# A four-layer graph kernel: new planned costs for TensorE's mode changes, and a new set of priorities for its planner

## The chip, the cores and the metric

The kernel runs on one core of one Trainium2 chip. The metric is the device time of one launch in microseconds (us). A core has five engines that run their own instruction streams and wait for one another through semaphores: TensorE (PE; its weight loads are listed as PEld) multiplies matrices, VectorE (DVE) and ScalarE (ACT) work element by element, GpSimd (POOL) does small work and issues DMAs, SyncE (SP) issues DMAs.

## The reference

32 independent graphs of 512 nodes with 256 features pass through four layers. Each layer is `x = layernorm(x + layer(x, adj))`:

- Layer 0: `h = (1+eps)*x + adj @ x`, then `relu(h @ W1 + b1) @ W2 + b2` with 512 hidden features.
- Layer 1: attention with 4 heads of 64 features. The score is `leaky_relu(e_dst[i] + e_src[j])` where `adj > 0.5`, masked elsewhere; softmax; times `h = x @ W`; plus a bias.
- Layer 2: attention with 8 heads of 32 features, `softmax(q k^T / sqrt(32) + log(adj + 1e-6))` times `v`, then an output projection with bias.
- Layer 3: `softmax` over nodes of `((x @ W) @ x^T) * adj` with a node mask, times `x`.

Everything is float32; 512 nodes are four chunks of 128, 256 features are two chunks of 128.

## The kernel before

**Tiling.** Each graph is computed by some 375 small steps, each with a name, an engine and a planned duration. In layer 0 they are `at` (adj transposed by TensorE, L679), `h` (adj @ x, L712), `f` and `y` (the two products of the layer, L735, L754). In layer 1: `xt1` (x transposed, L782), `v1` (L803), `z` (ACT, L906) and `zm` (DVE, L917) that make the weights, `o1` (weights times values, L940), `ad` (the four chunks of the weights added up by accumulating DMAs that POOL issues, L968), `d1` (the denominators out of them, L988), `yt`, `dt` (small transposes, L1017, L1018, L1005). In layer 2: `q`, `k` (L1073), `v2` (L1091) with its eviction `ve2` (ACT, L1097), `s` (scores of four heads at once, L1110), `e` (exponentials on ACT, L1123), `m` (times adj, DVE, L1132), `cd` (accumulating DMAs, L1143), `n` (weights times values of four heads at once, L1168), `d2` (denominators, L1198), `p` (projection, L1253). In layer 3: `i` (L1297), `t` (L1311), `te` (exponentials, L1341), `u` (transposes, L1350), `w` (L1365). The additions of biases to x are `xb` (POOL, L581), the reciprocal roots of the layer norms `dev` (POOL, L607). `la` and `lb` are the loads of adj for layer 0 and for layer 3.

**Modes of TensorE.** Most steps use the whole 128 x 128 array. Some use parts of it at the same time: `s` splits the rows in four (mode "row", 32 rows each), `n`, `d2` and `d1` split the columns in four (mode "c32"), `o1` splits the columns in two (mode "c64"). The others have mode "".

**Order.** The order of all instructions of all engines comes from a planner that runs while the program is built (class `Plan`). It replays the steps of all graphs with planned durations, and at each turn looks for those that could start first. Among the steps that can start within `ahead` of the earliest it takes the one with the smallest due time:

```
due = turn[g] * period - self.left[g][name] + moved[name] + stay * change
```

`left` is the planned length of the longest chain that follows the step, `period` is 28 (us per graph), `moved` holds shifts of single kinds of steps in us (before: the sum of 14 seeded random draws that each touch some 15% of the kinds), and `change` is the planned duration of the change of mode in front of a TensorE step, from the table `CHANGE`, weighted by `stay`. Up to six graphs (`window`) are in work at a time. Buffers are limited by a stock: 11 big tiles, 12 middle ones, 17 strips, and the eight PSUM banks ("p": 8), of which one `s` step takes four. What the planner hands out is only an order and a buffer for each tile: on the chip every engine runs its stream in that order, and semaphores hold an instruction until its operands are there. Planned times have no effect on the chip beyond the order and the choice of buffers.

Of the kernel before, what the change touches and what calls it, by code (L numbers as in the profile page):

```python
# [46 lines left out]
class Plan:  # L47
# [6 lines left out]

    HOP = {"pe": 0.2, "act": 0.15, "dve": 0.13, "pool": 0.05, "sp": 0.05}
    BACK = {"act": 0.13, "dve": 0.12}

    CHANGE = {  # L60
# [4 lines left out]
    }  # L65

    def __init__(self, stock):
# [64 lines left out]
            t = max(t, ends[h][n] + self.hop(self.steps[h][n], s))  # L132
        return t

    def order(self, period, ahead, window, stay, shifts=(), rush=()):


        room = {b: [(0.0, i) for i in range(n)] for b, n in self.stock.items()}
        engine, mode, out, last = {}, "", [], 0.0
        held = [{} for _ in self.steps]  # L140
        ends = [{} for _ in self.steps]
        waits = [{n: len(s.after) for n, s in steps.items()} for steps in self.steps]
        fwaits = [[len(after) for _, after in frees] for frees in self.frees]
        ready, low, opened = {}, 0, 0
        todo = [len(steps) for steps in self.steps]
        moved = dict.fromkeys((n for steps in self.steps for n in steps), 0.0)
        turn = [max(g - 1, 0) for g in range(len(self.steps))]
        for i, early in enumerate(rush):
            turn[-1 - i] -= early
        for seed, far in shifts:  # L150
            rng = random.Random(seed)
            for n in moved:
                if rng.random() < 0.15:
                    moved[n] += rng.uniform(-far, far)

        def open_to(n):
            nonlocal opened
            while opened < min(n, len(self.steps)):
                for name in self.steps[opened]:
                    if not waits[opened][name]:  # L160
                        ready[opened, name] = self.ready(opened, name, ends)
                opened += 1

        open_to(window)
        while low < len(self.steps):
            found = []
            for (g, name), t in ready.items():
                s = self.steps[g][name]
                t = max(t, engine.get(s.eng, 0.0))
                change = self.CHANGE[mode][s.mode] if s.eng == "pe" else 0.0  # L170
                for k, (kind, _, rest) in enumerate(s.take):
                    r, n = room[kind], sum(b[0] == kind for b in s.take[:k])
                    if len(r) <= rest + n:
                        break
                    t = max(t, r[n][0])
                else:
                    due = turn[g] * period - self.left[g][name] + moved[name] + stay * change
                    found.append((t, due, g, name, change))
            if not found:
                return math.inf, out  # L180
            first = min(found)[0] + ahead
            _, t, g, name, change = min((due, t, *f) for t, due, *f in found if t <= first)
            s = self.steps[g][name]
            t += change
            if s.eng == "pe":
                mode = s.mode
            del ready[g, name]
            got = {}
            for kind, key, _ in s.take:
                got[key] = held[g][key] = (kind, room[kind].pop(0)[1])  # L190
            if s.eng:
                engine[s.eng] = t + s.us
            end = ends[g][name] = t + s.us
            last = max(last, end)
            out.append((g, name, t, got))
            for h, n in s.then:
                waits[h][n] -= 1
                if not waits[h][n] and h < opened:
                    ready[h, n] = self.ready(h, n, ends)
            for k in s.frees:  # L200
                fwaits[g][k] -= 1
                if not fwaits[g][k]:
                    key, after = self.frees[g][k]
# [21 lines left out]
def fast_path(  # L225
# [102 lines left out]
    def prepare():  # L328
# [23 lines left out]
        def transposed(name, w):  # L352
            def raw():
                t[f"raw{name}"] = mid(f"raw{name}", [P, DC, D])
                return t[f"raw{name}"], rows(w)

            load(f"raw{name}", 2.0, raw, take=(f"C=raw{name}",))

            @step(f"wt{name}", "pe", 0.44, (f"raw{name}",), take=(f"p=wt{name}",))
# [12 lines left out]
            @step(f"we{name}", "act", 0.49, (f"wt{name}",), free=(f"wt{name}",))  # L372
            def _():
                nc.scalar.copy(wT[name].rearrange("p c f -> p (c f)"), t[f"wt{name}"])
# [36 lines left out]
                    prod.rearrange("p c (h f) -> p c h f", h=H1), AX.X, ALU.add,  # L411
                )

        @step("wtg", "pe", 0.44, ("wg",), take=("p=wtg",))
# [139 lines left out]
    def graph(g):  # L554
# [111 lines left out]
        for c in range(NC):  # L666

            @step(
                f"at{c}", "pe", 0.44, (f"la{c}",) + prev("at", c),
                take=(f"p=at{c}",) + (() if c else ("AT=ATcap", "B=AT/4", "D=ATd")),  # L670
            )
            def _(c=c):
                if c == 0:
                    t["AT"] = big("AT", [P, NC, N], "AT")

                    t["ATd"] = strip("ATd", [P, NC, P], "ATd")
                pt = t[f"pt{c}"] = bank(f"at{c}", [P, NC, P], f"AT_t_{c}")
                for m in range(NC):
                    nc.tensor.transpose(pt[:, m, :], t[f"A{c}"][:, blk(m)], ident)  # L679
# [88 lines left out]
        for d in range(DC):  # L768

            @step(  # L770
                f"xt1{d}", "pe", 0.44, row("r1", NC) + prev("xt1", d),
                take=(f"p=xt1{d}",) + (() if d else ("L1", "C=xT1/1")),
            )
            def _(d=d):
# [267 lines left out]
        def features_first(n, more=()):  # L1042
            for d in range(DC):

                @step(
                    f"xt{n}{d}", "pe", 0.44, row(f"r{n}", NC) + prev(f"xt{n}", d),
                    take=(f"p=xt{n}{d}",) + (() if d else (f"C=xT{n}",) + more),
                )
                def _(d=d):
# [49 lines left out]
        def scores(k):  # L1099
            o, c = divmod(k, NC)  # L1100

            @step(
                f"s{k}", "pe", 0.87, (f"qe{o}", f"ke{o}") + prev("s", k),
                take=tuple(f"p=s{k}{j}" for j in range(4)), mode="row",
            )
            def _():
# [49 lines left out]
        def attend(k):  # L1156
            o, c = divmod(k, NC)

            @step(
                f"n{k}", "pe", 0.87,  # L1160
                (f"m{k}1",) + ((f"n{k-1}",) if k else row("qe", 2) + row("ke", 2) + row("ve2", NC)),
                take=(f"p=n{o}",) if c == 0 else (), mode="c32",
            )
# [141 lines left out]
        for c in range(NC):  # L1305
# [37 lines left out]
                    accum_out=t["den"][:, c : c + 1],  # L1343
                )

            @step(f"u{c}", "pe", 0.44, (f"te{c}",) + prev("u", c), take=(f"p=u{c}",), free=(f"z3{c}",))
# [63 lines left out]
    for g in range(B):  # L1410
        graph(g)
    with tc.manual_schedule():
        plan.run([(28, 0.05, 6, 75.0, ((824592, 5.0), (893565, 10.0), (244737, 10.0), (911503, 5.0), (695937, 2.0), (23294, 5.0), (391254, 2.0), (207664, 2.0), (760101, 2.0), (339516, 5.0), (335230, 2.0), (34898, 2.0), (376325, 5.0), (379301, 2.0)), (0.6, 0.0, 0.1))])

# [470 lines left out]
```

## Time and profile before

| | us |
|---|---|
| median of 3 runs | 2972.07 (2971.11 to 2972.57) |
| profiled execution | 2974.01 |
| its span, first to last instruction | 2972.2 |
| granted TensorE clock, mean | 0.997 |
| busy: TensorE, DVE, ACT, POOL | 2929.2, 2127.1, 1918.8, 776.0 |

The profile shows one execution. Busy time of an engine is the time in which it has an instruction running; idle time of an engine is listed with what ended it. L735 is line 735 of the kernel. An operation in float32 of TensorE stands as two records for each matmul of the program, and records of matmuls in parts of the array start some nanoseconds apart and run together. The ends of matmuls are modelled, so the distance from one start to the next is the better measure of their pace.

### The profile page before, as it was taken

What the parts mean: (1) busy time and instruction counts of PE and PEld (TensorE: products, weight loads), DVE (VectorE), ACT (ScalarE), POOL (GpSimd) and SP (SyncE); (2) the same over time, 40 slices, a digit from 0 to 9 for tenths busy, and PEclk for the clock granted to TensorE, in tenths of its full rate; (3) what the DMA queues carried; (4) which work ended last, traced back from release to release, by engine and by line L of the source; (5) the groups of instructions that cost most, each with busy time, mean ns of one, the idle gap of its engine ahead of it and who ended that gap; (6) DMA issues with size and microseconds to landing.
All of it is one profiled execution on the core that took longest, in us unless ns stands there. A gap on an engine that the chain in (4) does not pass through costs nothing.

```text
span 2972.2 us, 42591 instructions
## 1 busy us (share of the span) xinstructions
PE 2929.2 (99%) x15521; PEld 1662.6 (56%) x15521; DVE 2127.1 (72%) x4133; ACT 1918.8 (65%) x3818; POOL 776.0 (26%) x688
## 2 busy tenths in 40 slices
PE   8899999999999999999999999999999999999998
PEld 6445555555555555555555555555565555555444
DVE  2577767776777777777767677767777776766886
ACT  3665766657666667666566666576666675656664
POOL 1333222232222222222222222222222222222220
PEclk9999999999999999999999999999999999999999
DMA  4677576676766676866777766768666766766770
GB/s 145 133 165 169 147 164 139 154 155 162 175 145 139 149 176 151 177 134 151 151 170 167 151 142 153 167 153 181 137 147 142 178 159 135 162 133 141 165 156 19
DMA packets 153368, 448.93 MB, mean 151 GB/s; under 512 B 15232, under 2 KB 55360, under 8 KB 125248
## 3 DMA queue, kind: packets, MB, share of 16 engines
q0 software_dynamic: 63648, 295.73, 52.3%
q1 hardware_dynamic: 88112, 149.75, 15.0%
q8 instruction: 125, 2.05, 0.3%
q10 hardware_dynamic: 1392, 0.66, 0.1%
q14 instruction: 91, 0.75, 0.1%
HBM read 133.30 MB, written 17.07 MB: 51 GB/s over the span
## 4 chain that ended last, share of the span: by engine, by line
PE 91%; DVE 3%; ACT 3%; DMA 2%; issue 1%; POOL 0%; POOLq 0%; ACTq 0%
PE s L1110 9%; PE h1T_ps L735 8%; PE o_ps L1168 8%; PE o_ps L940 7%; PE hT_ps L712 7%; PE o_ps L1365 7%; PE s L1311 7%; PE y_ps L754 7%; PE v_ps L803 4%; PE iT_ps L1297 4%; PE o2p_ps L1253 4%; PE v_ps L1091 4%; PE qT_ps L1073 3%; PE kT_ps L1073 3%; PE d_ps L1198 2%; PE eT_t L1350 2%
## 5 line engine op out<-in xcount | busy, mean ns | idle before, releaser
L1132 DVE SCALAR_TENSOR_TENSOR z<-AT,z 128x1024 f32<-128x1024 f32 x512 | 621.5, 1229 | 235.1 <-ACT z L1123 232.3
L1123 ACT ACTIVATE z<-s 128x512 f32<-128x512 f32 x1024 | 571.2, 606 | 99.2 <-PE s L1110 98.4
L917 DVE SCALAR_TENSOR_TENSOR z<-z,T,edge 128x512 f32<-128x512 f32 x512 | 412.4, 857 | 10.6 <-ACT z L906 10.1
L906 ACT ACTIVATE z<-R_bc,nT,S 128x512 f32<-128x512 f32 x512 | 382.9, 807 | 8.9 <-DMA R_bc<-R_dram 5.2
L1143 POOL DMA_DIRECT2D z<-z x186 | 164.9, 919 | 785.2 <-PE o_ps L1168 211.9
L968 POOL DMA_DIRECT2D z<-z x256 | 227.1, 1063 | 472.7 <-DMA z<-z 239.6
L581 POOL TENSOR_TENSOR x<-x,bias_bc 128x1024 f32<-128x1024 f32 x96 | 238.9, 2489 | 382.0 <-PE hT_ps L712 160.3
L1217 DVE RECIPROCAL rdT<-rdT 128x256 f32<-128x256 f32 x128 | 215.5, 1723 | 166.7 <-ACT rdT L1210 166.6
L625 ACT ACTIVATE x<-x,shift,rstd 128x256 f32<-128x256 f32 x508 | 289.6, 599 | 19.6 <-DVE shift L615 19.6
L1110 PE MATMUL s<-qT,kT 32*128 32x512 f32 x2048 | 294.9, 638 | 1.1 <-DVE y L1023 0.6
L607 POOL TENSOR_TENSOR rstd<-ve,nhalf 128x4 f32<-128x4 f32 (+1 forms) x131 | 144.5, 1146 | 545.3 <-DVE ve L601 530.0
L1168 PE MATMUL o_ps<-z,v 128*32 128x512 f32 x2048 | 264.2, 601 | 0.3 <-DVE z L1132 0.3
L940 PE MATMUL o_ps<-z,v 128*64 128x512 f32 x1024 | 237.8, 603 | 8.7 <-DVE z L917 8.7
L735 PE MATMUL h1T_ps<-hT,w_sb 128*128 128x512 f32 x512 | 245.6, 605 | 0.1
L1365 PE MATMUL o_ps<-x,eT 128*128 128x256 f32 x1024 | 237.6, 380 | 1.4 <-ACT eT L1355 1.3
L1311 PE MATMUL s<-xT,iT 128*128 128x512 f32 x512 | 238.9, 599 | 0.0
L754 PE MATMUL y_ps<-w_sb,h1T 128*128 128x256 f32 x1024 | 226.3, 379 | 0.0
L1365 PEld LDWEIGHTS o_ps<-x,eT 128*128 128x128 f32 x1024 | 193.3, 190 | 55.2 <-issue 19.0
L584 DVE BATCH_NORM_STATS2 st<-x 128x6 f32<-128x256 f32 x508 | 211.8, 417 | 7.9
L1341 ACT ACTIVATE z<-z,nmax 128x512 f32<-128x512 f32 x128 | 92.4, 722 | 193.2 <-DVE nmax L1333 191.7
L754 PEld LDWEIGHTS y_ps<-w_sb,h1T 128*128 128x128 f32 x1024 | 194.2, 190 | 38.5 <-issue 12.7
L712 PE MATMUL hT_ps<-AT,x 128*128 128x384 f32 (+2 forms) x768 | 211.5, 385 | 0.0
(152 smaller groups left out, 4192.0 us busy)
## 6 DMA issues: line engine op xcount, KB each, us to landing
z<-z POOLq DMA_DIRECT2D x186, 1024.0 KB, 9.1
A<-in_adj_dram SPq DMA_DIRECT2D x256, 256.0 KB
z<-z POOLq DMA_DIRECT2D x128, 512.0 KB, 7.1
R_bc<-R_dram SPq DMA_DIRECT2D x32, 1024.0 KB
z<-z POOLq DMA_DIRECT2D x128, 256.0 KB, 5.2
x<-in_x_dram SPq DMA_DIRECT2D x32, 512.0 KB
out_dram<-x SPq DMA_DIRECT2D x31, 512.0 KB
nm<-in_nodemask_dram SPq DMA_DIRECT2D x32, 256.0 KB
```

The source lines that it names most:

```text
L712: nc.tensor.matmul(ph[:, cols], t["x"][:, m, blk(d)], moving, start=(k == 0), stop=(k == len(parts) - 1),)
L735: nc.tensor.matmul(ph, w1_sb[:, d, blk(f)], t["hT"][:, d, :], start=(d == 0), stop=(d == DC - 1))
L754: nc.tensor.matmul(py[:, j, :], t["h1T"][:, f, blk(2 * c2 + j)], w2_sb[:, f, :], start=(f == 0), stop=(f == HC - 1),)
L906: nc.scalar.activation(t[f"e{h}"][:, c, :], t["Rbc"][:, h, :], AF.Relu, bias=t["nT"][:, h, c : c + 1], scale=t["S"][:, h, c : c + 1],)
L917: nc.vector.scalar_tensor_tensor(z, z, t["T"][:, h, c : c + 1], t["edge"][:, c, :], op0=ALU.add, op1=ALU.mult)
L940: nc.tensor.matmul(po[j * F1 : (j + 1) * F1, :], t["v"][:, c, h * F1 : (h + 1) * F1], t[f"e{h}"][:, c, :], start=(c == 0), stop=(c == NC - 1),
L1110: nc.tensor.matmul(pk, t["k"][hs, o, blk(c)], t["q"][hs, o, :], start=True, stop=True)
L1123: nc.scalar.activation(t[f"E{k}"][:, j, :], t[f"ps{k}{j}"], AF.Exp, scale=QSCALE)
L1132: nc.vector.scalar_tensor_tensor(z, t["AT"][:, c, None, :].to_broadcast([P, 2, N]), ADJ_EPS, z, op0=ALU.add, op1=ALU.mult,)
L1168: nc.tensor.matmul(t[f"n{o}"][32 * j : 32 * j + 32, :], t["v2"][:, c, o * P + F2 * j : o * P + F2 * (j + 1)], t[f"E{k}"][:, j, :], start=( ...
L1311: nc.tensor.matmul(pt, t["iT"][:, d, blk(c)], t["xT3"][:, d, :], start=(d == 0), stop=(d == DC - 1),)
L1365: nc.tensor.matmul(py, t[f"eT{c}"][:, blk(m)], t["x"][:, m, :], start=(m == 0), stop=(m == NC - 1),)
```

## The change

Three things change, all of them inputs of the planner.

1. Planned durations. The table of changes of mode gets other values (0.13 to 0.10, 0.17 to 0.218 and so on); the packed steps `s`, `n` and `d2` are planned with 0.855 instead of 0.87 us, transposes of four chunks with 0.437 instead of 0.44.
2. `order` takes a further argument, `moves`: a list of step kinds and of shifts in us, which are added to `moved`. 308 kinds are in it.
3. The arguments of the one run: `ahead` 0.05 to 0.0, `stay` 75 to 55, ten of the 14 seeded draws are replaced, the head start of the last graphs is 0.5, 0, 0 periods instead of 0.6, 0, 0.1.

No instruction is added or removed, and no operand but the choice of buffers differs.

```diff
     CHANGE = {
-        "": {"": 0.0, "row": 0.13, "c32": 0.1, "c64": 0.1},
-        "row": {"": 0.17, "row": 0.1, "c32": 0.2, "c64": 0.2},
-        "c32": {"": 0.12, "row": 0.12, "c32": 0.0, "c64": 0.12},
-        "c64": {"": 0.12, "row": 0.12, "c32": 0.12, "c64": 0.0},
+        "": {"": 0.0, "row": 0.1, "c32": 0.1, "c64": 0.09},
+        "row": {"": 0.218, "row": 0.11, "c32": 0.218, "c64": 0.218},
+        "c32": {"": 0.13, "row": 0.12, "c32": 0.02, "c64": 0.14},
+        "c64": {"": 0.118, "row": 0.118, "c32": 0.067, "c64": 0.0},
     }
...
-    def order(self, period, ahead, window, stay, shifts=(), rush=()):
+    def order(self, period, ahead, window, stay, shifts=(), rush=(), moves=()):
...
+        for n, far in moves:
+            moved[n] += far
         for seed, far in shifts:
...
-                f"at{c}", "pe", 0.44, (f"la{c}",) + prev("at", c),
+                f"at{c}", "pe", 0.437, (f"la{c}",) + prev("at", c),
...
-                f"s{k}", "pe", 0.87, (f"qe{o}", f"ke{o}") + prev("s", k),
+                f"s{k}", "pe", 0.855, (f"qe{o}", f"ke{o}") + prev("s", k),
...
-                f"n{k}", "pe", 0.87,
+                f"n{k}", "pe", 0.855,
...
-                f"d2{o}", "pe", 0.87 * len(chunks),
+                f"d2{o}", "pe", 0.855 * len(chunks),
...
-        plan.run([(28, 0.05, 6, 75.0, ((824592, 5.0), (893565, 10.0), (244737, 10.0), (911503, 5.0), ...), (0.6, 0.0, 0.1))])
+        plan.run([(28, 0.0, 6, 55.0, ((824592, 5.0), (893565, 10.0), (244737, 10.0), (23294, 5.0), ...), (0.5, 0.0, 0.0), (
...
+('ad00', -62.0), ('ad01', -61.5), ('ad10', -77.0), ('ad11', -51.5), ('ad20', -67.0), ('ad21', -32.5), ('ad30', -65.0), ('ad31', -48.0),
...
+('at1', -36.0),
...
+('e00', -46.5), ('e02', -5.0), ('e03', 10.0), ('e10', -34.0), ('e12', -1.0), ('e13', -2.0), ('e20', -1.0), ('e21', -9.0), ('e22', -95.0), ('e23', -32.0),
...
+('h0', -21.0), ('h1', -29.5),
...
+('i0', 27.5),
...
+('k0', -33.0),
...
+('la0i', -32.0), ('la1i', -33.5), ('la2i', 20.0), ('la3i', 2.0),
...
+('lb0i', -35.0), ('lb1i', -5.0), ('lb2i', -37.0), ('lb3i', -15.0),
...
+('o100', -38.5),
...
+('oe0', 21.5), ('oe1', 78.5),
...
+('s1', -36.0),
...
+('v23', -35.5),
...
+('ve10', 30.0), ('ve11', 10.0), ('ve12', 22.0), ('ve13', 31.5), ('ve20', 117.0), ('ve21', 58.0), ('ve22', 1.0), ('ve23', 6.5),
...
```

The same 0.44 to 0.437 stands at the other transposes (`wt`, `wtg`, `xt1`, `xt2`, `xt3`, `u`).

More of the change, by code (lines that the diff above doesn't have):

```diff
@@ L357, in transposed @@
             load(f"raw{name}", 2.0, raw, take=(f"C=raw{name}",))
-            @step(f"wt{name}", "pe", 0.44, (f"raw{name}",), take=(f"p=wt{name}",))
+            @step(f"wt{name}", "pe", 0.437, (f"raw{name}",), take=(f"p=wt{name}",))
             def _():
@@ L412, in _ @@
                 )
-        @step("wtg", "pe", 0.44, ("wg",), take=("p=wtg",))
+        @step("wtg", "pe", 0.437, ("wg",), take=("p=wtg",))
         def _():
@@ L770, in _ @@
             @step(
-                f"xt1{d}", "pe", 0.44, row("r1", NC) + prev("xt1", d),
+                f"xt1{d}", "pe", 0.437, row("r1", NC) + prev("xt1", d),
                 take=(f"p=xt1{d}",) + (() if d else ("L1", "C=xT1/1")),
@@ L1045, in _ @@
                 @step(
-                    f"xt{n}{d}", "pe", 0.44, row(f"r{n}", NC) + prev(f"xt{n}", d),
+                    f"xt{n}{d}", "pe", 0.437, row(f"r{n}", NC) + prev(f"xt{n}", d),
                     take=(f"p=xt{n}{d}",) + (() if d else (f"C=xT{n}",) + more),
@@ L1344, in _ @@
                 )
-            @step(f"u{c}", "pe", 0.44, (f"te{c}",) + prev("u", c), take=(f"p=u{c}",), free=(f"z3{c}",))
+            @step(f"u{c}", "pe", 0.437, (f"te{c}",) + prev("u", c), take=(f"p=u{c}",), free=(f"z3{c}",))
             def _(c=c):
@@ L1412, in fast_path @@
     with tc.manual_schedule():
-        plan.run([(28, 0.05, 6, 75.0, ((824592, 5.0), (893565, 10.0), (244737, 10.0), (911503, 5.0), (695937, 2.0), (23294, 5.0), (391254, 2.0), (207664, 2.0), (760101, 2.0), (339516, 5.0), (335230, 2.0), (34898, 2.0), (376325, 5.0), (379301, 2.0)), (0.6, 0.0, 0.1))])
+        plan.run([(28, 0.0, 6, 55.0, ((824592, 5.0), (893565, 10.0), (244737, 10.0), (23294, 5.0), (814168, 2.0), (264532, 2.0), (583369, 2.0), (708249, 5.0), (118144, 2.0), (603753, 2.0), (522046, 10.0), (973053, 5.0), (608632, 2.0), (603770, 2.0)), (0.5, 0.0, 0.0), (('Rl.q', 5.0), ('Rli', -10.5), ('Rs.q', -4.5), ('Rsi', 8.0), ('Rt', -14.5), ('ST', 4.5), ('ab', -6.0), ('ad00', -62.0), ('ad01', -61.5), ('ad10', -77.0), ('ad11', -51.5), ('ad20', -67.0), ('ad21', -32.5), ('ad30', -65.0), ('ad31', -48.0), ('aq00', 15.5), ('aq01', -16.0), ('aq10', 1.5), ('aq11', 2.5), ('aq20', -5.0), ('aq21', -5.0), ('aq30', 19.5), ('aq31', 61.0), ('at0', -1.5), ('at1', -36.0), ('at2', -12.0), ('at3', 8.5), ('atd0', 12.0), ('atd1', 5.0), ('atd2', -1.5), ('atd3', 6.5), ('ate0', 9.0), ('ate1', -57.5), ('ate2', 11.0), ('ate3', -0.5), ('cd1', -20.0), ('cd2', -16.5), ('cd3', -23.0), ('cd5', -10.0), ('cd7', -10.0), ('cq1', 6.0), ('cq2', -4.5), ('cq3', -55.5), ('cq6', -9.0), ('cq7', -15.0), ('d1', 4.5), ('d20', -2.5), ('d21', -4.5), ('de', -3.0), ('dev2.0', -11.0), ('dev4.0', -18.0), ('dt', -3.5), ('e00', -46.5), ('e02', -5.0), ('e03', 10.0), ('e10', -34.0), ('e12', -1.0), ('e13', -2.0), ('e20', -1.0), ('e21', -9.0), ('e22', -95.0), ('e23', -32.0), ('e30', -52.0), ('e31', -24.5), ('e32', -8.5), ('e33', 1.0), ('e42', -36.5), ('e43', -2.0), ('e50', -2.0), ('e51', -44.5), ('e53', -78.5), ('e60', -60.0), ('e61', -38.5), ('e62', -20.0), ('e63', -26.0), ('e70', -17.0), ('e71', -45.0), ('e72', -77.0), ('e73', -5.0), ('ed0', 46.5), ('ed1', 13.5), ('ed2', -19.5), ('ed3', 2.5), ('f0', 12.0), ('f1', 15.0), ('f3', -1.5), ('fe0', -12.0), ('fe1', -15.5), ('fe2', -8.0), ('fe3', 3.5), ('h0', -21.0), ('h1', -29.5), ('he0', -1.0), ('he1', 13.0), ('hsb.q', -1.0), ('hsbi', -2.0), ('hsl', -7.0), ('i0', 27.5), ('i1', 5.5), ('ie0', -1.0), ('ie1', 13.5), ('k0', -33.0), ('k1', 1.5), ('ke0', -10.0), ('ke1', 14.0), ('la0.q', 2.0), ('la0i', -32.0), ('la1.q', -32.5), ('la1i', -33.5), ('la2.q', -8.0), ('la2i', 20.0), ('la3.q', -3.0), ('la3i', 2.0), ('lb0.q', -44.0), ('lb0i', -35.0), ('lb1.q', 5.0), ('lb1i', -5.0), ('lb2.q', -33.0), ('lb2i', -37.0), ('lb3.q', -27.0), ('lb3i', -15.0), ('ldn.q', 3.0), ('ldni', -12.0), ('lx.q', 10.0), ('m00', -2.0), ('m01', 23.5), ('m10', 28.0), ('m20', 18.0), ('m21', -24.5), ('m30', 24.0), ('m31', 6.5), ('m40', 1.5), ('m41', -5.5), ('m50', 18.0), ('m51', -6.5), ('m60', 13.0), ('m61', 12.0), ('m70', 2.0), ('m71', 8.0), ('n0', 3.5), ('n1', 1.0), ('n2', -8.5), ('n4', 4.5), ('n5', -18.0), ('n6', -1.5), ('n7', 6.0), ('nd0', 16.0), ('nd1', -13.0), ('no0', 15.0), ('no1', 5.5), ('node', 11.5), ('o100', -38.5), ('o101', -4.5), ('o110', 3.0), ('o111', 5.5), ('oe0', 21.5), ('oe1', 78.5), ('out0.q', 7.0), ('out0i', 12.0), ('p0', 4.0), ('p1', -0.5), ('q0', 8.0), ('q1', 2.5), ('qe1', 2.0), ('r10', 1.0), ('r11', 15.0), ('r12', 81.5), ('r13', 10.0), ('r20', -12.5), ('r21', -15.5), ('r22', -4.0), ('r30', 2.0), ('r31', 46.0), ('r33', 4.5), ('r40', 42.5), ('r42', -15.5), ('r43', 4.5), ('rc00', 21.0), ('rc01', 0.5), ('rc10', 13.5), ('rd30', -10.0), ('rd32', 3.0), ('rd33', 2.0), ('s0', -1.5), ('s1', -36.0), ('s2', -2.0), ('s3', 0.5), ('s4', 14.0), ('s5', 3.5), ('s6', 6.5), ('s7', 8.5), ('sh1.0', 4.0), ('sh2.0', -31.5), ('sh3.0', 2.0), ('sh4.0', -3.0), ('st10', -1.0), ('st11', 13.5), ('st12', 24.5), ('st20', -7.5), ('st21', -8.0), ('st22', 7.0), ('st31', -3.0), ('st32', 3.0), ('st33', -8.5), ('st40', 6.0), ('st41', -6.5), ('st42', 6.5), ('st43', 20.5), ('t0', -7.0), ('t2', -8.5), ('t3', 0.5), ('ta0', -1.0), ('ta2', -3.0), ('ta3', -8.0), ('tb0', 4.0), ('tb1', 3.5), ('tb2', -10.5), ('tb3', 20.0), ('te1', -26.0), ('te2', -21.5), ('te3', 10.0), ('u0', 0.5), ('u1', -1.0), ('u2', -8.5), ('u3', -0.5), ('ue0', 1.5), ('ue1', 2.0), ('ue3', 22.0), ('v10', 8.0), ('v12', 10.0), ('v13', -1.5), ('v20', 1.0), ('v21', 1.5), ('v22', -14.5), ('v23', -35.5), ('va1.0', -19.0), ('va3.0', -0.5), ('ve10', 30.0), ('ve11', 10.0), ('ve12', 22.0), ('ve13', 31.5), ('ve20', 117.0), ('ve21', 58.0), ('ve22', 1.0), ('ve23', 6.5), ('w0', -2.0), ('w1', 2.0), ('w2', -17.0), ('w3', 5.5), ('wx0', -2.0), ('wx1', -1.0), ('wx2', -2.0), ('wx3', -15.5), ('x10', 4.5), ('x11', -10.0), ('x30', -22.0), ('x31', -13.0), ('xb1', -45.5), ('xb3', 2.0), ('xe10', 2.0), ('xe11', -61.5), ('xe20', -20.5), ('xe21', -8.5), ('xe30', 6.5), ('xe31', 3.5), ('xs.q', -1.5), ('xsi', 9.0), ('xt10', 9.5), ('xt20', 0.5), ('xt30', -2.0), ('xt31', -9.5), ('y0', 2.0), ('y1', -5.5), ('yd00', -21.0), ('yd01', 0.5), ('yd10', 10.5), ('yd11', -12.5), ('yn0', 7.5), ('yn1', 20.0), ('yn2', 26.0), ('yn3', 6.5), ('yt1', -3.0), ('yt2', -9.5), ('yt3', 5.5), ('z00', 9.5), ('z01', 4.5), ('z02', -18.0), ('z03', 51.0), ('z10', -2.0), ('z11', 3.0), ('z12', -1.0), ('z13', 31.0), ('z20', -2.0), ('z21', -21.0), ('z22', 45.0), ('z23', -4.0), ('z30', 40.0), ('z31', 3.0), ('z32', -27.5), ('z33', 10.0), ('zm00', -52.0), ('zm01', -4.5), ('zm10', -2.0), ('zm11', 7.0), ('zm20', -19.5), ('zm21', 7.5), ('zm30', -7.5), ('zm31', 2.0)))])
```

## The prediction

> **What bounds the kernel now.** I read the busy shares first.
>
> ```profile
> PE 2929.2 (99%) x15521; PEld 1662.6 (56%) x15521; DVE 2127.1 (72%) x4133; ACT 1918.8 (65%) x3818; POOL 776.0 (26%) x688
> ```
>
> TensorE (PE) is busy for 2929.2 of 2972.2 us. The change adds and removes no instruction, so DVE (72%), ACT (65%) and POOL (26%) matter only where they make TensorE wait. Next, stretches of the span (length; busy time of PE, PEld, DVE, ACT, POOL; clock, DMA share, GB/s).
>
> ```profile
> core 0: us, PE busy (x) PEld busy (x) DVE busy (x) ACT busy (x) POOL busy (x), PEclk, DMA share, GB/s
> 0.00:133.00 133.00, 116.09 (x565) 78.17 (x565) 57.89 (x153) 68.18 (x130) 35.89 (x40) 0.97 0.50 138
> 404.30:494.80 90.50, 90.32 (x485) 51.47 (x483) 65.93 (x129) 59.77 (x120) 24.08 (x22) 1.00 0.70 156
> 1490.00:1580.50 90.50, 90.32 (x485) 51.47 (x483) 65.95 (x129) 59.88 (x120) 24.04 (x22) 1.00 0.71 156
> 2665.00:2972.20 307.20, 292.93 (x1552) 154.71 (x1550) 229.72 (x442) 190.10 (x385) 63.75 (x58) 0.99 0.53 118
> ```
>
> From 404 to 2485 us the kernel repeats itself every 90.5 us, one graph per period, with TensorE idle for 0.18 us of it. Thirty-two periods are 2896 us; the other 76 us are the filling and the draining of the pipeline, where TensorE is idle for 16.9 of the first 133 us and for 14.3 of the last 307. The waits of TensorE, over the whole span, name the places (waited in total, times, longest):
>
> ```profile
> PE o_ps L940 <- DVE z L917: 8.7, 2, 8.1
> PE AT_t L679 <- DMA A<-in_adj_dram: 7.7, 2, 4.7
> PE AT_t L679 <- DVE rd L1010: 4.4, 24, 0.2
> PE d_ps L1198 <- DMA z<-z: 3.9, 1, 3.9
> PE iT_ps L1297 <- ACT xT L1058: 3.2, 3, 2.7
> ```
>
> Only the third recurs, once per period; the others are at the two ends. A busy TensorE is not a TensorE at its best pitch, though. The timeline of TensorE (start, length, what) shows what a change of array mode costs:
>
> ```profile
> 1504.87 1.92 PE L1168 MATMUL o_ps<-z,v 128*32 128x512 f32 x16
> 1506.72 1.14 PE L1110 MATMUL s<-qT,kT 32*128 32x512 f32 x8
> 1507.80 1.98 PE L735 MATMUL h1T_ps<-hT,w_sb 128*128 128x512 f32 x4
> 1509.71 1.14 PE L1110 MATMUL s<-qT,kT 32*128 32x512 f32 x8
> ```
>
> From start to start, 16 records of L1168 (four at a time) take 1.85 us, 8 of L1110 take 1.08 and 4 of L735 take 1.91; the same 4 of L735 inside full-array work take 1.72 in the chain of work that ended last. In the records the dense start-to-start distance of 512 columns is 0.429 us, of 256 columns 0.216, of 128 columns 0.109. At these, the work begun in 1490 to 1580.5 is 85.6 us. The excess is 4.84 us: 0.35 is the late start at L679, 1.15 lies inside packed steps and small operations, which no order changes, and 3.33 goes with 25 changes of mode (2.59 at the change itself, 0.09 to 0.11 each; 0.74 as a second bubble of about 0.1 us after a return to the full array). A change is therefore worth 3.33/25 = **0.133 us**, and one change per graph 32 times that, 4.3 us.
>
> **What the Trainium skill says.** "TensorEngine Tiling (Array Packing)", Key Properties: a change of tiling mode drains TensorE. The trace agrees: L1110 to L735 starts 0.52 us after the last group, not 0.43. "TensorE: Matmul & The Clock Gate", Architectural detail: ScalarE and VectorE take their queues strictly in order; in Step-by-step it says that matmuls stay in program order. So a planned order is binding, and a late operand holds everything behind it; L940 above, held for 8.1 us, shows this. The same page, What's actually happening: an idle window of about 3.4 us halves TensorE's clock. The trace has the granted clock at half from 123.1 us for 6.8 us, after that wait, and three times for 3.4 us near the end.
>
> **The change, part by part.** *Planned durations.* With the period's own changes (7 row to full, 4 full to c32, 4 c32 to row, 3 full to row, 2 c32 to full, 2 full to c64, and row to c32, c64 to c32, c64 to row once each) the old table plans 3.34 us, the new one 3.55, and measured are 3.33. Eighteen packed steps are planned 0.015 us shorter (-0.27) and five c32 neighbours 0.02 dearer (+0.10). The net is +0.04 us per graph, and the 0.003 us off a transpose is nothing: the planner's view hardly moves, and these numbers do no work on the chip. Cost 0.
>
> *Weight of a change in the due time.* It falls from 75 to 55. For the period's 25 changes 75 x 3.34 = 250 becomes 55 x 3.55 = 195: a fifth less reluctance to change. The chip pays only if more changes follow: from 0 to +3 per graph, 0 to +13 us. I take it together with the moves.
>
> *Moves of 308 step kinds, and new random shifts.* Kinds on TensorE move little (s, n, t, u, w, y on average by 5 or less; h0, h1, s1, k0, o100, v23, at1 by -21 to -39, i0 by +28). The large moves are elsewhere. The eight additions by DMA of layer 1 (ad) come 32 to 77 earlier, the exponentials of layer 2 (e) 28 earlier on average, the evictions of v (ve) and o1 (oe) 34 and 50 later, the loads of adj 11 and 23 earlier. Each, with its price: an ad issue takes POOL 1.08 us (L968) and is put ahead of a bias addition (2.47 us) or rstd (1.14 us); cover is POOL's 74% idle time, and without it the layer norm is late by 1.1 us per issue passed, then the transposes behind it. Its transfer, on the one software queue (52% of 16 engines), passes those of L1143 (9.1 us to landing). TensorE waits for any of them once only, near the end (the 3.9 us at L1198). An exponential (606 ns) put ahead frees its PSUM bank sooner, and the scores need four of eight banks; a v eviction (373 ns) pays by as much. Cover is ACT's 30.7 us of idle time per period; the planner never leaves a free engine waiting for a step of better due time beyond the small allowance, so a later due time means the next gap, whatever its size. Earlier loads on SP pass the other transfers there, 15 in all per graph on a queue with 15% of the 16 engines' span; a passed row transfer (R, xs) is late by the issues ahead of it, and TensorE waits for none of these in the periodic part. What can be gained: TensorE's waits and changes of mode.
>
> Sum for the likeliest case, against the profiled execution (2974.01 us; span 2972.2, 1.8 around it): (a) 0.35 us late start at L679: all of it is 23 x 0.35 = 8 us; I take half, -4. (b) changes of mode: no view shows the new order. Six visits to c32 for eleven c32 steps leave room to merge, and a merge saves two changes; more than two merges per graph would need all the banks at once. Between +3 and -4 per graph I take -2, one merge: -2 x 0.133 x 32 = -8.5. (c) the ends: the 8.1 us at L940 and half of the 6.8 us of half clock after it are 11.5, the waits at L1198, L1297 another 7, so up to -18; but an end has other chains close behind (DVE's norm of graph 0 was itself busy until 111 us), so -8. Together -20.5: 2953.5 us. The median of the runs stands 1.9 below the profiled execution, so **2952 us**, 0.7% faster.
>
> **Rivals.** *The order is as good as the old one* (2966 to 2978): TensorE is at 99%, waits for 0.18 us per period, and nothing done to ACT, DVE or POOL can bring more than that back. For it: steady state has no wait to remove. Against: 76 us at the ends and 3.33 us of changes per graph are all a matter of order, and a new order of this size hits neither exactly.
>
> *Slower through more changes of mode.* The weaker weight lets due times break up visits; place: TensorE's sequence within a graph. Price 4.3 us per change per graph; +3 gives 2972 + 12.8 = 2985. It decides from +1.4 per graph if nothing else is gained. Against: the moves sit on the same due times and can compensate.
>
> *Slower through late evictions.* ve20 and ve21 move by 117 and 58, four and two graphs' worth of due time (28 each). Every attend step waits, through n0, for all four v evictions, and behind n0 stands all of TensorE. If ACT then stands in a burst of layer 1's 16 activations (806 ns each), n0 is late by anything from 0 to 12.9 us; cover is whatever TensorE does before it. One wait of 0.7 us per graph makes 22 us, 2994; it decides at (20.5 + 6)/32 = 0.8 us per graph if the gains above come too, and at 0.2 if they do not. For it: the 0.18 us shows that the margins were used up with nothing to spare at L679. Against: ACT's 34% of idle time, in many gaps.
>
> **How the numbers follow.** A measurement of this kernel can tell about 0.2% (6 us) from no change. Likeliest case, faster: 0.58, its own range 2932 to 2966 holding 0.53 and 0.05 below that, since -4 changes (-17), all of L679 (-8) and all of the ends (-18) come to 2929. No change: 0.13. More changes: 0.10, at 2978 to 2990. Late evictions: 0.19, of which 0.11 lie above 2994. The range 2932 to 2994 leaves out 0.16. Faster 0.58, same 0.13, slower 0.29.
>
> **What would show it.** Right: a period under 90.2 us with fewer than 25 changes of mode per graph, the recurring wait of L679 on L1010 gone, TensorE idle less than 16.9 us in the first 133. Wrong in (b): 25 or more changes. Wrong in (a): a recurring wait of TensorE on ACT (v, L1097, or xT, L1058), DVE or DMA of more than 0.2 us per period. Wrong in (c): first or last stretch longer with the period unchanged. The prediction as a whole fails if the period passes 90.7 us.

## The result and the profile after

The changed kernel takes 2972.03 us (median of 12 runs, 2971.16 to 2974.47), the kernel before 2972.39 in the runs beside it: a ratio of 0.9999 with a 95% interval of 0.9990 to 1.0008. No difference can be measured. The forecast, 2952 us, was 20 us too low: a gain of 20 us was forecast and none came.

Under the equal sums lie two large and opposite differences. The first view below has the busy shares of the changed kernel, the second its stretches (length; busy time of PE, PEld, DVE, ACT, POOL; clock, DMA share, GB/s):

```profile
PE 2943.3 (99%) x15521; PEld 1668.0 (56%) x15521; DVE 2150.4 (72%) x4133; ACT 1927.3 (65%) x3818; POOL 801.4 (27%) x688
```

```profile
0.00:133.00 133.00, 121.50 (x590) 82.29 (x590) 57.88 (x150) 68.05 (x128) 38.38 (x43) 0.99 0.51 141
478.50:569.80 91.30, 91.18 (x483) 51.78 (x483) 66.73 (x128) 60.03 (x119) 24.89 (x21) 1.00 0.68 155
...
2662.20:2969.40 307.20, 299.36 (x1611) 161.62 (x1609) 233.72 (x458) 193.83 (x392) 68.06 (x60) 0.99 0.55 122
```

The period is 91.3 us, where it was 90.5. TensorE is busier in the first 133 us (121.5 us, before 116.1) and in the last 307 (299.4, before 292.9), and busier in total, though it computes the same. These are its waits over the whole span (waited in total, times, longest; the line numbers are higher than before by 3):

```profile
PE AT_t L682 <- DMA A<-in_adj_dram: 7.1, 2, 4.7
PE s L1113 <- ACT qT L1082: 2.9, 2, 2.1
PE o_ps L943 <- DVE z L920: 2.4, 2, 1.6
...
PE o_ps L1171 <- DVE z L1135: 0.6, 2, 0.4
```

The wait that recurred once per period (AT_t on rd) is gone, as are those of the end, and no recurring one is listed in its place. The next table splits the span at the ends of the last matmul of layer 3 of single graphs (counted from 0), in us:

| | before | after | difference |
|---|---|---|---|
| to the end of graph 1 | 385.2 | 387.2 | +2.0 |
| from there to graph 24, 23 periods | 2080.9 | 2100.4 | +19.5 |
| from there to the last matmul of graph 31 | 498.1 | 474.3 | -23.8 |
| after that, to the end of the span | 8.0 | 7.5 | -0.5 |
| span | 2972.2 | 2969.4 | -2.8 |

The end of the span won 24 us, and the periods lost some 0.8 us each. Where a period lost it is told by the chain of work that ended last: its shares by engine, and one place of it in order of time (start, us, what).

```profile
PE 85%; DVE 13%; DMA 1%; ACT 0%; issue 0%; POOL 0%; POOLq 0%; SPq 0%; ACTq 0%
```

```profile
1581.31 2.03 DVE ve L604
1583.34 1.12 DVE z L1135
1584.46 0.08 DVE ve L604
1584.54 0.33 DVE edge L897
1584.87 1.14 DVE z L1135
...
1588.30 1.14 DVE z L1135
1589.44 0.04 issue
1589.48 1.05 PE o_ps L1171 x4
1590.53 1.09 PE v_ps L806 x4
```

DVE had 3% of the chain before, and now has 13%. The chain goes through an operation on 128 x 4 elements, L604 (it adds a constant to the variances of a layer norm), that takes 2.03 us; the timeline of DVE has 0.15 us for the next one of the same line. These are the timelines of POOL and of TensorE at the same time:

```profile
1580.95 2.36 POOL L584 TENSOR_TENSOR x<-x,bias_bc 128x1024 f32<-128x1024 f32 x1 [8.39 <-PE xT_t L785]
```

```profile
1588.34 2.20 PE L1171 MATMUL o_ps<-z,v 128*32 128x512 f32 x8
```

L604 begins 0.36 us after POOL has begun a bias addition (`xb2`) and ends when that ends. DVE makes no pause from there to the product L1135 that ends at 1589.44. The `n` step at 1588.34 needs two such products, one for each pair of heads. Its first two heads start, and the other two, in the same step, start at 1589.48. So the step takes 2.12 us to the start of L806 at 1590.46. Since the first two heads are running meanwhile, TensorE is listed as busy.

### The profile page after: what moved, and what is told of

Same layout as the page of the kernel before. It is cut to its first block, busy times and chain, and to the rows that moved or that the text cites. A ratio compares the mean times of both kernels' runs of the same rounds, so it can differ in the third digit from the quotient of the medians.

```text
span 2969.4 us, 42791 instructions
## 1 busy us (share of the span) xinstructions
PE 2943.3 (99%) x15521; PEld 1668.0 (56%) x15521; DVE 2150.4 (72%) x4133; ACT 1927.3 (65%) x3818; POOL 801.4 (27%) x688
## 4 chain that ended last, share of the span: by engine, by line
PE 85%; DVE 13%; DMA 1%; ACT 0%; issue 0%; POOL 0%; POOLq 0%; SPq 0%; ACTq 0%
PE h1T_ps L738 8%; PE s L1314 8%; PE hT_ps L715 8%; PE o_ps L1368 7%; PE y_ps L757 7%; PE o_ps L1171 6%; PE s L1113 6%; PE o_ps L943 5%; DVE z L1135 4%; PE v_ps L806 4%; PE v_ps L1094 4%; PE iT_ps L1300 4%; PE kT_ps L1076 4%; PE qT_ps L1076 4%; DVE st L587 2%; PE d_ps L1201 2%
## 5 line engine op out<-in xcount | busy, mean ns | idle before, releaser
L1126 ACT ACTIVATE z<-s 128x512 f32<-128x512 f32 x1024 | 551.3, 605 | 250.2 <-PE s L1113 250.0
L1135 DVE SCALAR_TENSOR_TENSOR z<-AT,z 128x1024 f32<-128x1024 f32 x512 | 625.6, 1241 | 95.7 <-ACT z L1126 93.0
L920 DVE SCALAR_TENSOR_TENSOR z<-z,T,edge 128x512 f32<-128x512 f32 x512 | 416.8, 857 | 38.2 <-ACT z L909 38.1
L909 ACT ACTIVATE z<-R_bc,nT,S 128x512 f32<-128x512 f32 x512 | 376.6, 807 | 31.6 <-PE y_ps L757 22.4
L584 POOL TENSOR_TENSOR x<-x,bias_bc 128x1024 f32<-128x1024 f32 x96 | 245.2, 2555 | 395.0 <-PE xT_t L785 247.3
L628 ACT ACTIVATE x<-x,shift,rstd 128x256 f32<-128x256 f32 x508 | 296.9, 600 | 52.1 <-DVE shift L618 51.5
L1171 PE MATMUL o_ps<-z,v 128*32 128x512 f32 x2048 | 295.3, 603 | 3.6 <-DVE z L1135 0.6
L1113 PE MATMUL s<-qT,kT 32*128 32x512 f32 x2048 | 288.1, 634 | 2.9 <-ACT qT L1082 2.9
L943 PE MATMUL o_ps<-z,v 128*64 128x512 f32 x1024 | 250.0, 609 | 2.7 <-DVE z L920 2.4
L610 POOL TENSOR_TENSOR rstd<-ve,nhalf 128x4 f32<-128x4 f32 (+1 forms) x131 | 169.7, 1298 | 289.5 <-DVE ve L604 286.9
L1113 PEld LDWEIGHTS s<-qT,kT 32*128 32x128 f32 x2048 | 87.2, 183 | 170.3 <-ACT z L1126 74.9
```

Source lines behind the costliest of these rows:

```text
L909: nc.scalar.activation(t[f"e{h}"][:, c, :], t["Rbc"][:, h, :], AF.Relu, bias=t["nT"][:, h, c : c + 1], scale=t["S"][:, h, c : c + 1],)
L920: nc.vector.scalar_tensor_tensor(z, z, t["T"][:, h, c : c + 1], t["edge"][:, c, :], op0=ALU.add, op1=ALU.mult)
L943: nc.tensor.matmul(po[j * F1 : (j + 1) * F1, :], t["v"][:, c, h * F1 : (h + 1) * F1], t[f"e{h}"][:, c, :], start=(c == 0), stop=(c == NC - 1),
L1113: nc.tensor.matmul(pk, t["k"][hs, o, blk(c)], t["q"][hs, o, :], start=True, stop=True)
L1126: nc.scalar.activation(t[f"E{k}"][:, j, :], t[f"ps{k}{j}"], AF.Exp, scale=QSCALE)
L1135: nc.vector.scalar_tensor_tensor(z, t["AT"][:, c, None, :].to_broadcast([P, 2, N]), ADJ_EPS, z, op0=ALU.add, op1=ALU.mult,)
```

## The experiments

**Moving the bias addition, and nothing else.** In the list that the planner hands out, `xb2` of each graph is put behind `ad11` of the same graph.

```diff
-        for g, name, _, got in self.order(*best[1])[1]:
+        out = self.order(*best[1])[1]
+        for name, mark in (('xb2', 'ad11'),):
+            for g in range(len(self.steps)):
+                if name in self.steps[g]:
+                    at = next(i for i, s in enumerate(out) if s[:2] == (g, name))
+                    step = out.pop(at)
+                    at = next(i for i, s in enumerate(out) if s[:2] == (g, mark))
+                    out.insert(at + 1, step)
+        for g, name, _, got in out:
```

> The changed kernel with one move in the emitted order: POOL's bias addition xb2 of a graph is issued directly behind the DMA issue ad11 of the same graph, some 66 planned us later than before, at a place where DVE is idle; x needs it only about 100 planned us after its old place. Nothing else is moved. Theory A (the addition holds up DVE): in the changed kernel L604, a 0.16 us operation, takes about 2.0 us once per graph because POOL's xb2 runs at the time; DVE then works without a pause until it delivers the second half of one n step's weights 1.1 us late, and TensorE stands for it in the middle of that step. Expected: L604 at 0.16 us everywhere in the periodic part, the n step whole again, the period 91.31 -> 90.1 to 90.4 us, the time 2935 to 2948 us. Theory C (DVE is late because its planned durations are too short, 1.14 planned for 1.22 us of L1135, wherever xb2 stands): L604 short, but the n step still split, 2966 to 2974 us.

Measured: 2939.42 us, a ratio of 0.9882 (0.9866 to 0.9899) to the kernel before, which took 2973.94 us beside it. That is 33 us less than the changed kernel takes. The next lines are the groups of the small DVE operation, first in the changed kernel, then in this one (busy, mean ns | idle before):

```profile
L604 DVE TENSOR_SCALAR ve<-mv 128x4 f32<-128x4 f32 (+1 forms) x131 | 71.9, 549 | 1.3
```

```profile
L612 DVE TENSOR_SCALAR ve<-mv 128x4 f32<-128x4 f32 (+1 forms) x131 | 20.8, 159 | 1.3
```

In the changed kernel 27 of the 131 take over 1 us, 2.04 on average; here none does. The period is 90.16 us, which is 1.15 less. The `n` step, in the timeline of TensorE:

```profile
1480.60 1.04 PE L1179 MATMUL o_ps<-z,v 128*32 128x512 f32 x8
1481.58 0.71 PE L814 MATMUL v_ps<-wg_sb,xT 128*128 128x264 f32 x2
```

It takes 0.98 us from start to start instead of 2.12. These 1.14 us make up the difference of the periods, and from 478 to 2400 us no wait of TensorE is listed. Theory A holds, and theory C falls, since the step is whole. This version beats both kernels.

The expectation was wrong in one point: DVE is not idle at the new place. There the addition meets L1285 (`node`, which turns the node mask into numbers). The first line is the group of L1285, the others are from the timelines of DVE and POOL.

```profile
L1285 DVE TENSOR_SCALAR nonode<-nm 128x512 f32<-128x512 int32 x32 | 90.6, 2830 | 0.0
...
1540.88 3.45 DVE L1285 TENSOR_SCALAR nonode<-nm 128x512 f32<-128x512 int32 x1
1546.63 1.75 DVE L1228 RECIPROCAL rdT<-rdT 128x256 f32<-128x256 f32 x1 [2.31 <-ACT rdT L1221]
...
1541.37 2.66 POOL L592 TENSOR_TENSOR x<-x,bias_bc 128x1024 f32<-128x1024 f32 x1
```

In the changed kernel the same line has a mean of 417 ns; here 26 of the 32 take over 1 us, and they keep DVE busy for 77 us more, against the 51 that L604 is spared. Behind L1285 DVE still has a pause of 2.31 us. So the 33 us did not come from sparing DVE work, but from the place at which DVE is held up.

A second experiment asks whether the late product is the loss or the split of the step. It turns the order of the heads in the changed kernel.

```diff
-                for j in range(4):
+                for j in (2, 3, 0, 1):
                     nc.tensor.matmul(
                         t[f"n{o}"][32 * j : 32 * j + 32, :],
```

> The changed kernel with the four heads of every n step in the order 2, 3, 0, 1: the first matmul then waits for the later half of the weights, and all four always run at the same time. Theory A (the wait for DVE is the loss, the first pair runs inside it): within 0.2% of the changed kernel, 2966 to 2978 us; the wait becomes visible as about 1.1 us of idle TensorE per graph on L1171 <- DVE L1135. Theory B (the loss is that two pairs run one after the other where four heads could run at once): about 1.1 us per graph less, 2935 to 2942 us.

Measured: 2972.81 us, 0.9996 (0.9987 to 1.0004). The wait now shows (waited in total, times, longest):

```profile
PE o_ps L1171 <- DVE z L1135: 28.2, 29, 1.2
```

28.2/29 is 0.97 us each time. Theory B falls: running the two pairs one after the other cost nothing of its own, since the first pair filled a wait. The wait was there in the changed kernel and could not be seen, because the first half of the step hid it.

**The parts of the change.** One run has the new planned durations alone, with the old arguments of the run. The next has the change without the list of moves.

```diff
-        plan.run([(28, 0.0, 6, 55.0, (...), (0.5, 0.0, 0.0), (('Rl.q', 5.0), ...))])
+        plan.run([(28, 0.05, 6, 75.0, (...), (0.6, 0.0, 0.1))])
```

> The kernel before with the new planned durations (table of mode changes, 0.855 and 0.437) alone, its own ahead, stay, draws and head starts, no moves. The prediction's step: cost 0, the planner's view hardly moves: 2966 to 2978 us, 25 changes of mode per graph. Rival (the order of a list planner hangs on ties, and draws chosen for one table do not suit another): the order is a different one, without the strict period, 3010 to 3060 us.

Measured: 3054.55 us, 1.0262 (1.0245 to 1.0279). The rival came true: the intervals between graphs swing between 72 and 121 us, and there are 940 changes of mode where the kernel before has 824.

```diff
-        plan.run([(28, 0.0, 6, 55.0, (...), (0.5, 0.0, 0.0), (('Rl.q', 5.0), ...))])
+        plan.run([(28, 0.0, 6, 55.0, (...), (0.5, 0.0, 0.0))])
```

> The changed kernel without the list of 308 moves; new durations, stay 55, ahead 0, the new draws and head starts stay. If the moves carry what the change gains at the end of the span (the last seven graphs 24 us shorter): the end as long as before or longer, 3000 to 3040 us in all. If the draws and the lower stay carry it: 2965 to 2985 us. In either case L604 is not expected to meet xb2 again, since only the moves bring the two together.

Measured: 3080.28 us, 1.0357 (1.0339 to 1.0374), above both expectations, with 943 changes of mode, periods of 92.2 to 96.2 us after the first few graphs, and 519 us for the last seven graphs instead of 474. Without the moves the new values are 3.6% worse than the old kernel; the moves bring that back, and the end besides. One part of the expectation held: L604 meets `xb2` no longer once per graph (one of its 131 operations takes over 1 us). At 0.133 us each, the prediction's price, the 116 and 119 more changes of these two runs make 15 to 16 us. The rest of their loss, 65 and 90 us, was not taken apart.

**The end of the span.** The changed kernel with the old head starts.

```diff
-(0.5, 0.0, 0.0), (('Rl.q', 5.0), ...
+(0.6, 0.0, 0.1), (('Rl.q', 5.0), ...
```

> The changed kernel with the old head starts of the last graphs (0.6, 0, 0.1 periods instead of 0.5, 0, 0); all else as changed, so the periodic part keeps its order. It asks whether the 24 us won at the end come from the moves alone or need the head starts that were chosen with them. Moves alone: 2970 to 2974 us. Both together: the period unchanged at 91.3 us, the end 8 to 20 us longer, 2980 to 2992 us.

Measured: 2992.45 us, 1.0062 (1.0045 to 1.0078). The period is the same 91.31 us, and the last seven graphs take 494.1 us instead of 474.3. So 20 of the 24 us are lost with the old head starts, and the run without the moves, which has the new head starts, took 519 us there. As far as these two runs show, both are needed. The traces of before and after account for a part of the 24: TensorE is idle for 19.0 us of the last 506 before and for 8.1 of the last 482 after, and the three stretches of half clock (3.4 us each, so some 5 us lost) are gone. The remaining 8 us were not traced to single waits.

**Does each hold-up of DVE cost time?** The hold-up of L1285 above says no. In the kernel of the first experiment another bias addition, `xb3`, also holds up L928 (layer 1's masking), by 58 us in all. It was moved away too, first to a place that turned out badly chosen. The edits are shown against the first experiment.

```diff
-        for name, mark in (('xb2', 'ad11'),):
+        for name, mark in (('xb2', 'ad11'), ('xb3', 'cd3')):
...
-                if name in self.steps[g]:
+                if name in self.steps[g] and mark in self.steps[g]:
```

> The kernel of e1 with a second bias addition moved in the same way: xb3 of a graph behind the DMA issue cd3 of the same graph, where DVE is idle. In e1 xb3 still holds up one L920 operation (zm of layer 1) by 1.95 us per graph, 58 us over the span. Theory A with slack (a hold-up of DVE costs only where DVE has no pause left before the next operand TensorE waits for): the stretched L920 operations vanish, DVE is busy some 1.9 us less per graph, TensorE's period stays 90.16 us, the time 2936 to 2942 us. Rival (every hold-up of DVE costs time): 0.5 to 1.2 us less per graph, 2900 to 2925 us.

Measured: 2949.05 us, 0.9918 (0.9901 to 0.9934), 10 us slower than without the second move; neither expectation holds. At the new place `xb3` meets another small operation, and the groups show the exchange:

```profile
L928 DVE SCALAR_TENSOR_TENSOR z<-z,T,edge 128x512 f32<-128x512 f32 x512 | 364.8, 755 | 39.2 <-ACT z L917 39.1
L626 DVE SCALAR_TENSOR_TENSOR shift<-mv,rstd 128x4 f32<-128x4 f32 (+1 forms) x131 | 85.2, 651 | 26.9 <-POOL rstd L618 26.9
```

L626 takes 3.25 us in 21 graphs, and the period is 90.30 us instead of 90.16. L1285 happens to be free here (a mean of 439 ns), so DVE is held up for less time in all than in the first experiment, and the kernel is slower all the same. The hold-up of L626, longer than that of L604, went with 0.14 us per period; the other 6 us came with a few single intervals of up to 93.9 us, which were not traced. A better place for the same question follows.

```diff
-        for name, mark in (('xb2', 'ad11'), ('xb3', 'cd3')):
+        for name, mark in (('xb2', 'ad11'), ('xb3', 'cd7')):
```

> The kernel of e1 with xb3 of a graph behind the DMA issue cd7 of the same graph, where DVE works on two reciprocals of 1.7 us that read nothing else (behind cd3, in e5, xb3 met the small operation L626 instead, which then took 3.1 us in 21 graphs). L928 is no longer held up (58 us less busy DVE) and nothing else is. Theory A with slack: the period stays 90.16 us and the time within 0.2% of e1's 2939.4, 2934 to 2945 us. Rival (each hold-up of DVE costs time): 1 us per graph less, 2900 to 2925 us.

Measured: 2940.16 us, 0.9892 (0.9876 to 0.9909), like the first experiment.

```profile
L928 DVE SCALAR_TENSOR_TENSOR z<-z,T,edge 128x512 f32<-128x512 f32 x512 | 369.1, 764 | 39.7 <-ACT z L917 39.6
L626 DVE SCALAR_TENSOR_TENSOR shift<-mv,rstd 128x4 f32<-128x4 f32 (+1 forms) x131 | 20.4, 156 | 27.0 <-POOL rstd L618 27.0
```

DVE is spared 48 us of holding up at L928 (417.2 us in the first experiment, so most of the 58) and 13 at L1285, and the time is the same. Those hold-ups had cost nothing.

**The same in the kernel before.** There `xb2` begins as the small operation ends (0.13 us after its start), so the two do not collide. One run moves `xb2` away, with the lines of the first experiment and another mark. The other moves the small operation into it.

```diff
+        for name, mark in (('xb2', 'ad21'),):
...
```

> The kernel before with the same kind of move as e1: xb2 of a graph behind its DMA issue ad21, where DVE works on reciprocals. In the kernel before the small operation L601 has just finished when xb2 starts, and xb2 holds up one edge mask (L894) by 0.5 us per graph. Theory A: no gain beyond 0.2%, 2968 to 2978 us. Rival (xb2 at its old place costs in every order, the move of e1 is a gain of its own and not the undoing of what the change did): about 1.1 us per graph less, 2936 to 2945 us.

Measured: 2974.64 us, 1.0003 (0.9994 to 1.0011). The move is no gain of its own.

```diff
...
+        for g in range(len(self.steps) - 1):
+            if "va4.0" in self.steps[g] and "x31" in self.steps[g + 1]:
+                at = next(i for i, s in enumerate(out) if s[:2] == (g, "va4.0"))
+                to = next(i for i, s in enumerate(out) if s[:2] == (g + 1, "x31"))
+                if at < to < at + 12:
+                    out.insert(to, out.pop(at))
```

> The kernel before with one DVE operation of 0.15 us, va4.0 (L601), issued one step later, behind the residual addition x31 (0.68 us) of the next graph. In the kernel before it ends as xb2 starts on POOL; one step later it should fall into xb2. Nothing is added. Theory A: L601 takes 1.8 to 2.0 us once per graph, DVE runs 1.9 us late, uses up its pauses of 0.44 us, and delivers the weights of the n step that follows 0.7 to 1.0 us late: the period 90.48 -> 91.1 to 91.5 us, 2990 to 3005 us. Rival (the collision is harmless in an order that has more pauses on DVE, or a step's move by 0.7 us does nothing): 2968 to 2978 us.

Measured: 2973.19 us, 1.0003 (0.9994 to 1.0011): the expectation of a loss was wrong. The collision is there, in 27 operations of 1.93 us on average, and DVE's timeline shows why it costs nothing:

```profile
1568.95 1.95 DVE L608 TENSOR_SCALAR ve<-mv 128x4 f32<-128x4 f32 x1
...
1573.35 1.21 DVE L1139 SCALAR_TENSOR_TENSOR z<-AT,z 128x1024 f32<-128x1024 f32 x1
...
1574.58 1.23 DVE L1139 SCALAR_TENSOR_TENSOR z<-AT,z 128x1024 f32<-128x1024 f32 x1
1576.83 1.23 DVE L1139 SCALAR_TENSOR_TENSOR z<-AT,z 128x1024 f32<-128x1024 f32 x1 [1.02 <-ACT z L1130]
```

In the kernel before the three products start at 1572.49, 1574.23 and 1576.75. They are late by 0.86, 0.35 and 0.08 us. Pauses behind the collision take the delay up (and an edge mask that `xb2` had held up by 0.5 us is now clear of it), and a wait of 1.02 us for ACT is left before the third. I had reckoned with the 0.44 us pause alone. In these runs a collision costs what the pauses do not take up before the next operand that TensorE waits for.

**Shorter pieces.** In the last run the changed kernel has `xb2` at its old place, as four additions.

```diff
+                if k == 2:
+                    for c in range(NC):
+                        xc = t["x"][:, c, :]
+                        nc.gpsimd.tensor_tensor(xc, xc, bias_bc[:, 1, :], ALU.add)
+                    return
```

> The changed kernel with xb2 at its old place, as four additions of 256 columns instead of one of 1024. Theory A: L604 can wait for one quarter only, 0.6 us instead of 1.9; with DVE 1.3 us earlier the n step, late by 1.1 us, is whole again or nearly so: 2936 to 2950 us. If the quarters come between DVE's operations one after the other and hold each of them up in turn, the sum is the same as before: 2965 to 2975 us.

Measured: 2983.67 us, 1.0035 (1.0023 to 1.0048), slower still and above both expectations, with a period of 91.71 us. The first two lines are from POOL's timeline, the last is from DVE's.

```profile
1584.65 4.09 POOL L586 TENSOR_TENSOR x<-x,bias_bc 128x256 f32<-128x256 f32 x4 [7.77 <-PE xT_t L790]
1588.71 3.01 POOL L615 TENSOR_TENSOR rstd<-ve,nhalf 128x4 f32<-128x4 f32 x2
...
1590.76 0.16 DVE L623 SCALAR_TENSOR_TENSOR shift<-mv,rstd 128x4 f32<-128x4 f32 x1 [0.59 <-POOL rstd L615]
```

No DVE operation of the line of L604 takes more than 0.7 us now, but two per graph are held up. The four quarters take 4.09 us instead of 2.36: the third, which meets one of DVE's long products, takes 1.77 us, the others 0.72 to 0.98. The reciprocal roots queued behind them on POOL end later, and DVE waits for these. So a hold-up also runs the other way, from DVE to POOL.

## Why the prediction was wrong

**(a), the wait at L679: right.** It is gone. I took half of its 0.35 us per period; it was nearly all of it, since with `xb2` out of the way the period is 90.16 us, 0.32 less than before. The collision put 1.15 on top.

**(b), two fewer changes of mode per graph: wrong.** There are 25 per period before, after, and in the first experiment (824, 819 and 819 in all). The gain of 8.5 us, for which no view spoke, was zero.

**(c), the ends: right in kind, mis-sized.** I put -8 us and thought first of the wait of 8.1 us at L940. The start came out 2 us longer to graph 1, and the drain 24 us shorter. That wait is nearly gone (2.4 us at L943), and TensorE is idle for 11.5 of the first 133 us instead of 16.9, but its clock is granted at half for 10.2 us of the start instead of 6.8. I had also misread the half clock before: on the time of the other lines it begins at 111.9 us, within the wait, and not at 123.1 behind it. Only 3.5 of its 6.8 us are busy, so by the same reckoning it cost some 1.7 us and not 3.4.

**Cost 0 of the new planned durations: wrong as reasoned.** That they price the old sequence the same (+0.04 us per graph) is true and says little: the planner takes one step at a time, and with other prices it took another sequence, 2.6% slower by itself. A planner's inputs cannot be priced one by one by their sums.

**The covers: the step that failed.** This is the step at which the forecast broke. I priced what is moved on POOL as a queue: an `ad` issue ahead of a bias addition, an addition ahead of a root, with POOL's 74% idle time as cover, and I set DVE aside with "DVE (72%), ACT (65%) and POOL (26%) matter only where they make TensorE wait". The place of `xb2` in time against DVE's operations was not in the sum. It cost DVE 1.9 us in each of 27 graphs, of which 1.14 reached TensorE: 31 us, nearly all of the 33 that the first experiment gave back. With that one move the changed order takes 2939 us, 34.5 less than the kernel before beside it, so the gains were there, and more than the 20.5 of the sum. The prediction's own sign of failure, a period over 90.7 us, came.

**The rivals.** That 2972 lies within 2932 to 2994 was luck: gains and a loss of over 30 us each cancelled. "The order is as good as the old one" gave the right number and not the reason: nothing done to ACT, DVE or POOL was to bring more than the small waits back, and one POOL operation mattered by 33 us. "More changes of mode" did not come. "Late evictions" had the right form, a late operand at an `n` step with everything on TensorE behind it, and about the right size to decide (0.8 us per graph; 1.14 came), but the wrong operand: no eviction is late, the product of DVE is.

**The kernel before could have shown it.** These are two of its DVE groups:

```profile
L917 DVE SCALAR_TENSOR_TENSOR z<-z,T,edge 128x512 f32<-128x512 f32 x512 | 412.4, 857 | 10.6 <-ACT z L906 10.1
L601 DVE TENSOR_SCALAR ve<-mv 128x4 f32<-128x4 f32 (+1 forms) x131 | 23.3, 178 | 0.6
```

L917 has a mean of 857 ns, while most of its operations take 743 in the trace; the excess is 59 us in 29 operations that overlap a bias addition. The Trainium skill has a reason in "SBUF — State Buffer", Who interferes with whom: VectorE and GpSimd share a pair of ports to SBUF, the one that comes second is fully blocked until the first has ended, and it concerns VectorE operations with two inputs in SBUF, beside a GpSimd operation that reads SBUF, or in a fast mode that `tensor_scalar` can enter. The traces agree in which operations are held up by a bias addition: L604 (`tensor_scalar`) takes up to 2.3 us, L626 and L917 (two inputs in SBUF) up to 3.3 and 2.9, while statistics (0.4 us) and reciprocals (1.7) keep their length. In two points they do not show what the page says. The records of L626 and L1285 begin 0.6 and 0.5 us before that of the addition, yet end with it or shortly after. And 86 of the products at L1135 in the changed kernel, with two inputs in SBUF, begin during POOL's power operation, which reads SBUF too, and take their usual 1.21 us. Only the other way is it seen there: the power operation takes 1.56 us on average when it begins during an operation of L1135 or L920, and 0.98 when it meets none. No run shows the ports, or the mode of L604. The prediction did not draw on this section.

## What to carry to other kernels

When a new order of the same instructions brings nothing, compare the mean of each small operation between the two traces early: one line at 549 ns where it had 178 led here to nearly all of the loss. Then ask what stands behind it, since another line at 2830 ns where it had 417 cost nothing. A busy engine can hide a wait when a group of instructions runs in parts; putting the late operand first made it visible here at no cost that could be measured (2972.81 us). A planner that treats engines as independent can place POOL's long additions on DVE's path by chance. They are better placed beside operations that they did not hold up here (statistics, reciprocals), or in front of a pause.

## What the runs showed of the hardware

- An addition of 128 x 1024 on POOL (2.4 to 2.7 us) held up single DVE operations of 0.15 us for 1.9 us (L604) and 3.1 us (L626), and one of 0.42 us for 3.0 (L1285). The same small DVE operations beside POOL's power operation on 128 x 4 (1.0 to 1.1 us) were not lengthened.
- Cutting the addition into four made the pair worse: 4.09 us for POOL's part instead of 2.36, and 91.71 instead of 91.31 us per period.
- Four heads that share the array in columns start together or in pairs. While one pair waited for data the other ran: the step took 2.12 us instead of 0.98, and the profile listed no idle time.
